# Selective scan: B held in two buffers and loaded ahead of C, constants and delta weights loaded where they are used

## The chip, the cores and the metric

The kernel runs on one core of a Trainium2 chip. The core has a matrix engine (TensorE, PE in the profile; its loads of stationary operands are PEld), a vector engine (VectorE, DVE), an engine for activation functions (ScalarE, ACT), a general engine (GpSimd, POOL), and SyncE (SP), whose queue issues nearly all transfers here. Each engine works through its own instructions in order; semaphores tie them together. Transfers between the device's DRAM and on-chip memory (SBUF) run on 16 DMA engines. The metric is the time of one execution on the device in microseconds (us); the profile is of one separate execution.

## What is computed

The reference is a stack of four residual layers on a picture batch x of 8 x 64 x 64 x 96 (float32). Each layer adds to x a function of its group norm. Layers 0 and 2 are selective scans, layer 1 is a chunked scan with one decay per head, layer 3 is a filter (upsampling by a Fourier transform, a small polynomial network, low pass). The change concerns above all layers 0 and 2, which have the same form:

```python
xz = x @ in_proj_w.T;  xp, z = split(xz)            # 192 channels each
xc = silu(depthwise_conv3x3(xp) + conv_b)           # u, as 4096 positions
xs = [rows, columns, rows backwards, columns backwards] of xc       # K = 4 directions
dts, B, C = split(x_proj_weight[k] @ xs[k])         # 6, 16 and 16 rows
delta = softplus(dt_projs_weight[k] @ dts + bias)   # 192 channels
for l in positions:                                 # state h: 192 channels x 16
    h = exp(delta[l] * A) * h + (delta[l] * u[l]) * B[l]
    y[l] = sum over the 16 states of h * C[l]
out = (layernorm(sum over directions of y + D * u) * silu(z)) @ out_proj_w.T
```

## The kernel before

The images are worked through one after the other; between the layers only the residual goes to DRAM and back. A selective layer (`selective_scan`) does 32 steps, one for each of the 4 directions and 8 chunks of `LC` = 512 positions. A step has six units (`units`, the variable `n`): a unit is 32 channels times 4 of the 16 states on the 128 partitions, and the other 4 groups of states (`NSG`) lie one behind the other in the free dimension, so that its tiles are 128 x 2048.

For each unit:

- `enter` (ACT, L528) copies the last states of the chunk before into the edge of `db`.
- `spread` (PE, L536) repeats delta * u of 32 channels on 128 partitions, into the PSUM tile `pu`, of which there is one. Units 2 and 5 use `du2` instead, which came through DRAM.
- `with_b` (L542) multiplies by B: `db = pu * b` on DVE for units 0, 1, 3 and 4, `db = du2 * b` on POOL for units 2 and 5.
- `decays` (ACT, L557) computes exp(A * delta) from `dx` into the PSUM tiles `das`, two halves of two instructions each.
- `scan` (DVE, L572) is the recurrence, two instructions per unit.
- `leave` (L588, L593) copies the last state on ACT and multiplies `h` by C in place on POOL; POOL's product waits for the copy.
- `total_y` (PE, L600 and L610) sums over the states for three units at a time; ACT copies the sum into `y` (L701).

What a step needs is made ahead by the generator `prepare(i)`. Each `yield` ends one part, and `prepare_part` runs one part. Two products on PE (L448, L458) with the joined weights `wdts` give the raw delta, B and C; ACT copies them to SBUF (`raw1` L453, `raw0` L463). B and C go to DRAM (`bcd`, L465) and come back repeated on partitions: `copies` (L472) issues four transfers of 256 KB each for `c` and four for `b`. Softplus (L483) makes delta; `dd` (L493, L495) takes it to DRAM by halves, and `repeat` (L490) brings each half back as a `dx` tile, four transfers of 192 KB each. `dx` of half 0 serves units 0 to 2, that of half 1 units 3 to 5. POOL multiplies delta by u (`du`, L501), and `dud` (L504) and `du2` (L507) take a part of that through DRAM.

The order of the work in this stage is written out by hand (`tc.manual_schedule()`): each engine gets its instructions in the order in which the program names them. The main loop runs over all units `t`; while step i runs, the parts of step i+1 are called at these places: parts 1 and 2 already in units 4 and 5 of the step before, part 3 in unit 1, parts 4 (`bcd` and `c`) and 5 (softplus, the first `dd`, `dx` of half 0, the second `dd`) in unit 2, part 6 (`b`) in unit 3, part 7 (`du`, `dud`, `du2`) in unit 4, part 8 (`dx` of half 1) in unit 5. All transfers of a step stand in this order in SP's queue. A transfer that reads DRAM that another one wrote waits on SP until that one has landed, and what stands behind it waits too.

Buffers come in pools. Those of `chunk` (`cp`: `c`, `dx`) have two buffers, those of `soft` (`tp`: `raw0`, `raw1`, `b`, `du`, `du2`, `wdts`) have one. `wdts`, the weights of all four directions, is loaded from DRAM at the start of the stage; `wdt` is computed once at the start of the program.

`cst`, a table of constants of 128 x 1746, lies in SBUF for the whole program. It holds the matrices that the selective scan uses (`sel`, `red`, `ident`), that of the group norm (`group`), those of the chunked scan (`tris`, `past`, `heads`, `sel6`, `same`, `lw_fixed`) and the filters of layer 3 (`up`, `down`). The chunked scan copies `lw_fixed` into `lw` at its start (L738), on DVE and POOL. Outside of the parts that are ordered by hand a scheduler orders the instructions.

Of the kernel before, what the change touches and what calls it, by code (L numbers as in the profile page):

```python
# [17 lines left out]
DM = 96  # L18
NST = 16
RK = 6  # L20
# [26 lines left out]
K_SEL = 0  # L47
K_RED = K_SEL + 128
K_ID = K_RED + 32
K_TF = K_ID + 128  # L50
K_TB = K_TF + 128
K_UF = K_TB + 128
K_UB = K_UF + 128
K_GRP = K_UB + 128
K_UP = K_GRP + 96
K_DN = K_UP + 128
K_LW = K_DN + 64
K_DIA = K_LW + 2 * LWC
K_S6 = K_DIA + 6
K_BLK = K_S6 + 4 * 96  # L60
K_ALL = K_BLK + 192


@with_exitstack
def tile_vision_stack(
# [26 lines left out]
        nc.sync.dma_start(t, src)  # L92
        return t

    cst = resident("cst", consts, [128, K_ALL])
    w0s = resident("w0s", w0, [DM, C_ALL])
    a0s = resident("a0s", a0, [128, K * 24])
    w1s = resident("w1s", w1, [DM, C_ALL])
# [6 lines left out]
    sel = cst[:DM, K_SEL:K_RED]  # L105
    red = cst[:, K_RED:K_ID]
    ident = cst[:, K_ID : K_ID + 128]
    tris = (cst[:, K_TF : K_TF + 128], cst[:, K_TB : K_TB + 128])
    past = (cst[:, K_UF : K_UF + 128], cst[:, K_UB : K_UB + 128])
    group = cst[:DM, K_GRP : K_GRP + 96]  # L110
    up = cst[:64, K_UP : K_UP + 128]
    down = cst[:, K_DN : K_DN + 64]
    lw_fixed = cst[:, K_LW : K_LW + 2 * LWC].rearrange("p (i r) -> p i r", i=2)
    heads = cst[:, K_DIA : K_DIA + RK]
    sel6 = cst[:, K_S6 : K_S6 + 4 * 96].rearrange("p (j m) -> p j m", j=4)
    same = cst[:DM, K_BLK : K_BLK + 192]

    zero = wp.tile([128, NSG], F32, name="zero")
    nc.vector.memset(zero, 0.0)
# [285 lines left out]
    def selective_scan(w, wdt, a, d, u, y):  # L405
# [18 lines left out]
            for c in (range(NCH) if k < 2 else range(NCH - 1, -1, -1))  # L424
        ]
        units = NCG
        total = len(steps) * units
        with (
            tc.tile_pool(name="dram", bufs=2, space=DRAM) as dp,
# [10 lines left out]
            def prepare(i):  # L440

                k, c = steps[i]
                wh, at = k % 2 == 1, c * LC
                uv = [view(u[:, hf, :], wh, at, LC) for hf in range(2)]
                m = made[i] = {"dx": [], "du": []}
                pv = pyp.tile([128, LC], F32, name="pv", tag="py")
                for hi in range(2):
                    nc.tensor.matmul(  # L448
                        pv[:DM], wdts[:, k, hi, 128:], uv[hi], start=(hi == 0), stop=(hi == 1)
                    )  # L450
                yield
                raw1 = tp.tile([128, LC], F32, name="raw1")
                nc.scalar.copy(raw1[:DM], pv[:DM])  # L453
                yield

                pv = pyp.tile([128, LC], F32, name="pv", tag="py")
                for hi in range(2):
                    nc.tensor.matmul(  # L458
                        pv, wdts[:, k, hi, :128], uv[hi], start=(hi == 0), stop=(hi == 1)
                    )  # L460
                yield
                raw0 = tp.tile([128, LC], F32, name="raw0")
                nc.scalar.copy(raw0, pv)  # L463
                bcd = dp.tile([32, LC], F32, name="bcd")
                nc.sync.dma_start(bcd, raw0[DM:])  # L465

                def copies(at, pool, name):

                    t = pool.tile([128, NSG, LC], F32, name=name)
                    src = bcd[at : at + NST].rearrange("(g n) l -> n g l", n=4)  # L470
                    for n in range(4):
                        nc.sync.dma_start(  # L472
                            t[32 * n : 32 * n + 32],
                            src[n : n + 1].to_broadcast([32, NSG, LC]),
                        )
                    return t

                m["c"] = copies(NST, cp, "c")
                yield
                delta = [raw0[:DM], raw1[:DM]]  # L480
                for hf in range(2):
                    bias = w[:, C_DTB + 2 * k + hf : C_DTB + 2 * k + hf + 1]
                    nc.scalar.activation(delta[hf], delta[hf], AF.Softplus, bias=bias)  # L483
                dd = dp.tile([192, LC], F32, name="dd")

                def repeat(hf):
                    dx = cp.tile([128, 3, LC], F32, name="dx")
                    src = dd[hf * 96 : hf * 96 + 96].rearrange("(q c) l -> c q l", c=32)
                    for n in range(4):
                        nc.sync.dma_start(dx[32 * n : 32 * n + 32], src)  # L490
                    m["dx"].append(dx)

                nc.sync.dma_start(dd[:DM], delta[0])  # L493
                repeat(0)
                nc.sync.dma_start(dd[DM:], delta[1])  # L495
                yield
                m["b"] = copies(0, tp, "b")
                yield
                du = tp.tile([DM, 2, LC], F32, name="du")
                for hf in range(2):  # L500
                    nc.gpsimd.tensor_mul(cut(du[:, hf, :], wh), cut(delta[hf], wh), uv[hf])  # L501
                m["du"] = du
                dud = dp.tile([32, 2, LC], F32, name="dud")
                nc.sync.dma_start(dud, du[64:96])  # L504
                m["du2"] = du2 = tp.tile([128, 2, LC], F32, name="du2")
                for n in range(4):
                    nc.sync.dma_start(du2[32 * n : 32 * n + 32], dud)  # L507
                yield
                repeat(1)
# [115 lines left out]
                    next(going[i], None)  # L625


            wdts = tp.tile([DM, K, 2, 224], F32, name="wdts")
            nc.sync.dma_start(wdts, wdt)
            dg = cp.tile([128, NSG, LC], F32, name="c").rearrange("p a b -> p (a b)")  # L630
            dg = dg[:DM, : 18 * DM].rearrange("p (n m) -> p n m", n=18)
            diagonals(dg, w)
# [4 lines left out]
            with tc.tile_pool(name="p_conv", bufs=2, space=PSUM) as pvp:  # L637

                def conv_block(n):
                    acc = pvp.tile([DM, 2, LC], F32, name="acc")  # L640
                    for hf in range(2):
                        conv_pe(dg, y, n, hf, acc[:, hf, :])
                    return n, acc

                def silu_block(n, acc):
                    for hf in range(2):
                        silu(w, u, (8 * n, 8 * n + 8), hf, acc[:, hf, :])

                for hf in range(2):
                    conv(w, y, u, (0, 8), hf)  # L650
                for _ in range(5):
                    prepare_part(0)
                blocks = [conv_block(5)]
                conv(w, y, u, (8, 24), 0)
                for _ in range(3):
                    prepare_part(0)
                conv(w, y, u, (8, 24), 1)
                for _ in range(2):
                    prepare_part(1)
                blocks.append(conv_block(6))  # L660
                silu_block(*blocks[0])
                conv(w, y, u, (24, 40), 0)
                blocks.append(conv_block(7))
                silu_block(*blocks[1])
                conv(w, y, u, (24, 40), 1)
                silu_block(*blocks[2])
            with tc.tile_pool(name="p_da", bufs=1, space=PSUM) as pap:
# [11 lines left out]
                for t in range(total + 2):  # L679
# [31 lines left out]
                    if n == 2:  # L711
                        prepare_part(i + 1)
                        prepare_part(i + 1)
                    elif n == 3:
                        prepare_part(i + 1)
                    elif n == 5:
                        prepare_part(i + 1)
                        prepare_part(i + 2)

    def chunked_scan(w, d, u, y):  # L720

        xproj = w[:, C_XP : C_XP + K * 2 * XR].rearrange("p (k j r) -> p k j r", k=K, j=2)
        yr = y.rearrange("p j (h w) -> p j w h", w=64)
        with tc.tile_pool(name="both", bufs=1) as bo, tc.tile_pool(name="bcd", bufs=1, space=DRAM) as bdp:
            lw = bo.tile([128, 2, NQ, LWC], F32, name="lw")
            for i in range(2):
                (nc.gpsimd.tensor_copy if i else nc.vector.tensor_copy)(  # L738
                    lw[:, i, :, :], lw_fixed[:, i : i + 1, :].to_broadcast([128, NQ, LWC])
                )  # L740

            bts = [bo.tile([DM, 4 * Q], F32, name=f"bt{n}") for n in range(2)]
            for bt in bts:
                nc.gpsimd.memset(bt, 0.0)
            bcds = [bdp.tile([32, L], F32, name=f"bcd{k}") for k in range(K)]
            for o in range(2):
                with tc.tile_pool(name="order", bufs=1) as op:
                    chunked_order(o, w, d, xproj, u, y, yr, lw, bts, bcds, op)

    def chunked_order(o, w, d, xproj, u, y, yr, lw, bts, bcds, op):  # L750
        xt = op.tile([128, NQ, 192], F32, name="xt")
        xd = op.tile([128, NQ, 2, RK + NST], F32, name="xd")
        dt = op.tile([128, NQ, 2, RK], F32, name="dt")
# [331 lines left out]
    def spectral_layer(xd, sb, dst):  # L1085

        with tc.tile_pool(name="spec", bufs=1) as lp, tc.tile_pool(name="spec2", bufs=2) as sp:
            xs = load(lp, xd)
            xn = lp.tile([DM, L], F32, name="xn")
            xt = lp.tile([64, 64, DM], F32, name="xt", tag="turn")  # L1090
            x1 = lp.tile([64, 128, DM], F32, name="x1")
# [287 lines left out]
```

## Time and profile before

| | |
|---|---|
| median of 3 runs | 32874.29 us (32872.7 to 32905.18) |
| the profiled execution's own time | 32765.36 us |
| its span in the profile | 32763.6 us |
| instructions | 279135 |
| DVE busy | 24776.0 us, 76% |
| PE busy | 24399.9 us, 74% |
| POOL busy | 21606.8 us, 66% |
| ACT busy | 16308.8 us, 50% |
| moved by DMA | 2684.51 MB, 82 GB/s on average |
| granted TensorE clock | 0.726 |

The span is the time from the first to the last instruction of one profiled execution. An engine's busy time leaves out its waits. The profile also gives, for each group of equal instructions, the time that the engine stood idle just before them and what ended it (the releaser); a list of waits, summed over the program; the instructions in order of time; and the time from a transfer's issue to its landing. For transfers, what the timeline shows under SPq is the issue alone, not the movement of the data.

### The profile page before, as it was taken

Reading aid. Unit: us, or ns where it says so; the run is one execution under the profiler, and the core shown is the slowest. Engines: PE = TensorE matmul, PEld = TensorE weight load, DVE = VectorE, ACT = ScalarE, POOL = GpSimd, SP = SyncE. Lnnn points to the kernel's source line nnn. Section 1 sums busy time; section 2 is a strip of 40 time slices with the busy share of each in tenths; the row PEclk is TensorE's granted clock in tenths of the full one; section 3 lists DMA queues with packets and bytes.
Section 4 is the critical chain, followed back from the end, with each engine's and each line's share of the span. In section 5 each row is a group of like instructions: output and inputs, shape, how many; then the busy total and the mean of one; then the engine's idle time right before and its main releaser. Section 6 shows DMA issues by size and latency. Waiting matters only on the chain. (4 is left out here: it accounts for less than half of the span.)

```text
span 32763.6 us, 279135 instructions
## 1 busy us (share of the span) xinstructions
PE 24399.9 (74%) x90246; PEld 9157.0 (28%) x90246; DVE 24776.0 (76%) x17921; ACT 16308.8 (50%) x28493; POOL 21606.8 (66%) x8844
## 2 busy tenths in 40 slices
PE   6696866968669686696766967669676686866868
PEld 1241311413114131141321413114131241312413
DVE  8858688586885868858688586886868868687686
ACT  5435454354543545435454354543545435454354
POOL 8639487394863948639477394864948639486494
PEclk7676776767767677677776767767677676776767
DMA  4314243042430424304243042431424314243142
GB/s 115 88 27 119 63 112 88 25 119 65 112 88 24 121 65 112 88 23 121 65 108 92 23 121 65 112 88 27 119 64 112 88 27 121 62 115 85 28 121 61
DMA packets 1496292, 2684.51 MB, mean 82 GB/s; under 512 B 304601, under 2 KB 304825, under 8 KB 1494833
## 3 DMA queue, kind: packets, MB, share of 16 engines
q1 hardware_dynamic: 1478192, 2660.35, 32.6%
q8 instruction: 722, 11.83, 0.2%
q10 hardware_dynamic: 16640, 6.29, 0.1%
q14 instruction: 738, 6.04, 0.1%
HBM read 2282.63 MB, written 383.06 MB: 81 GB/s over the span
## 5 line engine op out<-in xcount | busy, mean ns | idle before, releaser
L572 DVE TENSOR_TENSOR_SCAN h<-da,db 128x1026 f32<-128x1026 f32 x6144 | 13651.3, 2278 | 210.0
L593 POOL TENSOR_TENSOR h<-h,c 128x2048 f32<-128x2048 f32 x3072 | 12784.8, 4169 | 620.3 <-ACT state L588 490.6
L536 PE MATMUL pu<-du,cst 32*128 32x512 f32 x4096 | 3574.0, 966 | 5275.1 <-DVE db L542 5222.9
L542 DVE TENSOR_TENSOR db<-pu,b 128x2048 f32<-128x2048 f32 x2048 | 4654.1, 2272 | 2062.5 <-DMA b<-bcd 2057.1
L557 ACT ACTIVATE da<-dx,a2s 128x512 f32<-128x512 f32 x6144 | 4237.7, 690 | 3657.5 <-DVE h L572 3177.7
L557 ACT ACTIVATE da<-dx,a0s 128x512 f32<-128x512 f32 x6144 | 4237.7, 690 | 3639.4 <-DVE h L572 3156.5
L542 POOL TENSOR_TENSOR db<-du,b 128x2048 f32<-128x2048 f32 x1024 | 4648.7, 4540 | 1705.4 <-PE pu L536 644.8
L610 PE MATMUL py<-h,cst 128*32 128x512 f32 x24576 | 5307.4, 801 | 61.0 <-POOL h L593 61.0
L536 PEld LDWEIGHTS pu<-du,cst 32*128 32x128 f32 x4096 | 869.7, 263 | 7680.6 <-DVE db L542 6472.7
L610 PEld LDWEIGHTS py<-h,cst 128*32 128x32 f32 x24576 | 1150.6, 143 | 4882.5 <-issue 4778.8
L448 PE MATMUL pv<-u,wdts 96*96 96x512 f32 x2048 | 1461.5, 841 | 1101.7 <-ACT state L588 567.6
L237 POOL TENSOR_SCALAR xn<-xs,sb 96x512 f32<-96x512 f32 x192 | 207.2, 1084 | 3141.4 <-DVE sb L217 2960.3
L950 ACT ACTIVATE sg<-sg 128x768 f32<-128x768 f32 x1024 | 819.2, 800 | 2446.8 <-PE sg L934 2446.8
L881 POOL TENSOR_TENSOR rr<-lr,cst 128x768 f32<-128x768 f32 x256 | 430.3, 1681 | 2346.0 <-ACT lr L879 1252.2
L458 PE MATMUL pv<-u,wdts 96*128 96x512 f32 x2048 | 1504.1, 864 | 585.2 <-ACT state L588 325.5
L600 PE MATMUL py<-y,cst 96*96 96x512 f32 x1536 | 1551.3, 1108 | 39.6 <-ACT state L588 39.6
L501 POOL TENSOR_TENSOR du<-raw,u 96x512 f32<-96x512 f32 x1024 | 1435.4, 1423 | 0.0
L982 DVE TENSOR_TENSOR wt<-wt,cbm 128x768 f32<-128x768 f32 x1024 | 1089.1, 1084 | 344.6 <-ACT wt L951 341.3
L1020 PE MATMUL py<-wt,xdt 128*32 128x128 f32 x12288 | 1020.1, 332 | 236.1 <-DVE y L1058 156.6
L1028 PE MATMUL py<-ce,state 96*96 96x128 f32 x3968 | 1119.1, 372 | 0.0
L1141 DVE SCALAR_TENSOR_TENSOR f<-p,w3bs,f 128x512 f32<-128x512 f32 x768 | 576.8, 751 | 714.3 <-ACT f L1134 687.7
L588 ACT COPY state<-h 128x4 f32<-128x4 f32 x3072 | 592.8, 193 | 1017.1 <-DVE h L572 1008.7
(210 smaller groups left out, 32009.2 us busy)
## 6 DMA issues: line engine op xcount, KB each, us to landing
dx<-dd SPq DMA_DIRECT2D x4096, 192.0 KB, 3.7
c<-bcd SPq DMA_DIRECT2D x2048, 256.0 KB, 4.9
b<-bcd SPq DMA_DIRECT2D x2048, 256.0 KB, 6.3
du<-dud SPq DMA_DIRECT2D x2048, 128.0 KB, 2.6
dd<-raw SPq DMA_DIRECT2D x1024, 192.0 KB, 5.1
dud<-du SPq DMA_DIRECT2D x512, 128.0 KB, 6.2
xd<-xs SPq DMA_DIRECT2D x256, 192.0 KB, 2.0
xs<-xd SPq DMA_DIRECT2D x128, 384.0 KB, 5.8
```

The costliest lines, as they stand in the source:

```text
L448: nc.tensor.matmul(pv[:DM], wdts[:, k, hi, 128:], uv[hi], start=(hi == 0), stop=(hi == 1))
L458: nc.tensor.matmul(pv, wdts[:, k, hi, :128], uv[hi], start=(hi == 0), stop=(hi == 1))
L501: nc.gpsimd.tensor_mul(cut(du[:, hf, :], wh), cut(delta[hf], wh), uv[hf])
L536: nc.tensor.matmul(pu, sel[rows, :], m["du"][rows, n // 3, :], start=True, stop=True)
L542: (nc.gpsimd if pool else nc.vector).tensor_mul(groups(m["db", n]), (m["du2"][:, n // 3, :] if pool else m["pu"]) .unsqueeze(1) .to_broadc ...
L557: nc.scalar.activation(dst[:, g, :LC], made[i]["dx"][n // 3][:, n % 3, :], AF.Exp, scale=av4[:, k, n, gs : gs + 1],)
L572: nc.vector.tensor_tensor_scan(made[i]["h", n][:, at][:, way], das[p][:, rev : 2 * SEG + rev][:, way], made[i]["db", n][:, at][:, way], 0. ...
L593: nc.gpsimd.tensor_mul(h, h, made[i]["c"])
L600: nc.tensor.matmul(py, skip[:, hf, :] if k == 0 else ident[:DM, :DM], view((u if k == 0 else y)[:, hf, :], wh, c * LC, LC), start=True, st ...
L610: nc.tensor.matmul(py[32 * q : 32 * q + 32, :], red, hs[q][:, g, :], start=False, stop=(g == NSG - 1),)
L982: nc.vector.tensor_mul(it["wt"], it["wt"], m["cbm"][:, j : j + 1, :].to_broadcast([128, RK, Q]),)
L1028: nc.tensor.matmul(py[:, i, hf, :], it["before"][:, 96 * hf : 96 * hf + 96], m["ce"][:, j, :], start=False, stop=True,)
```

## The change

There are three parts, which hang together through the space in SBUF.

B: `b` moves from the pool with one buffer to that with two, and its four transfers move from a part of their own (part 6) to part 4, ahead of those of `c`. `prepare` has seven parts instead of eight, so one call at the start of the stage and the call in unit 3 fall away; all other parts stay in the units where they were.

Delta weights: instead of one load of 672 KB with all four directions at the start of a stage, one direction of 168 KB is loaded at a time, into two buffers `wk`. The first is loaded in the first part of step 0, the others in the first part of steps 2, 10 and 18, each six steps before its first use.

Constants: `cst` keeps only the 384 columns that selective scan and group norm use. Those of the chunked scan (1170 columns) are loaded as `cc` at the start of each chunked scan, the filters (192 columns) as `filters` at the start of layer 3, after `xs`. The columns of the table are reordered for it.

```diff
-    cst = resident("cst", consts, [128, K_ALL])
+    cst = resident("cst", consts[:, :K_TF], [128, K_TF])
...
             def prepare(i):
...
+                if i in (0, 2, NCH + 2, 2 * NCH + 2):
+
+                    j = (i + NCH - 1) // NCH
+                    weights[j] = cp.tile([DM, 2, 224], F32, name="wk")
+                    nc.sync.dma_start(weights[j], wdt[:, j])
                 pv = pyp.tile([128, LC], F32, name="pv", tag="py")
                 for hi in range(2):
                     nc.tensor.matmul(
-                        pv[:DM], wdts[:, k, hi, 128:], uv[hi], start=(hi == 0), stop=(hi == 1)
+                        pv[:DM], weights[k][:, hi, 128:], uv[hi], start=(hi == 0), stop=(hi == 1)
                     )
...
+                m["b"] = copies(0, cp, "b")
                 m["c"] = copies(NST, cp, "c")
                 yield
...
                 nc.sync.dma_start(dd[DM:], delta[1])
-                yield
-                m["b"] = copies(0, tp, "b")
                 yield
                 du = tp.tile([DM, 2, LC], F32, name="du")
...
-            wdts = tp.tile([DM, K, 2, 224], F32, name="wdts")
-            nc.sync.dma_start(wdts, wdt)
...
                 conv(w, y, u, (8, 24), 0)
-                for _ in range(3):
+                for _ in range(2):
                     prepare_part(0)
...
                     if n == 2:
                         prepare_part(i + 1)
                         prepare_part(i + 1)
-                    elif n == 3:
-                        prepare_part(i + 1)
                     elif n == 5:
...
     def chunked_scan(w, d, u, y):
...
+            cc = bo.tile([128, K_UP - K_TF], F32, name="cc")
+            nc.sync.dma_start(cc, consts[:, K_TF:K_UP])
+            lw_fixed = cc[:, K_LW - K_TF : K_DIA - K_TF].rearrange("p (i r) -> p i r", i=2)
...
     def spectral_layer(xd, sb, dst):
...
             xs = load(lp, xd)
+            filters = lp.tile([128, 192], F32, name="filters")
+            nc.sync.dma_start(filters, consts[:, K_UP:])
+            up, down = filters[:64, :128], filters[:, 128:]
```

`chunked_order` takes `cc` as an argument and cuts `tris`, `past`, `heads`, `sel6` and `same` out of it, as was done with `cst`.

More of the change, by code (lines that the diff above doesn't have):

```diff
@@ L49 @@
 K_ID = K_RED + 32
-K_TF = K_ID + 128
+K_GRP = K_ID + 128
+K_TF = K_GRP + 96
 K_TB = K_TF + 128
@@ L53 @@
 K_UB = K_UF + 128
[L54 to L57, printed above, removed]
+K_LW = K_UB + 128
 K_DIA = K_LW + 2 * LWC
@@ L60 @@
 K_BLK = K_S6 + 4 * 96
-K_ALL = K_BLK + 192
+K_UP = K_BLK + 192
+K_DN = K_UP + 128
+K_ALL = K_DN + 64
 @with_exitstack
@@ L107, in tile_vision_stack @@
     ident = cst[:, K_ID : K_ID + 128]
-    tris = (cst[:, K_TF : K_TF + 128], cst[:, K_TB : K_TB + 128])
-    past = (cst[:, K_UF : K_UF + 128], cst[:, K_UB : K_UB + 128])
     group = cst[:DM, K_GRP : K_GRP + 96]
[L111 to L116, printed above, removed]
     zero = wp.tile([128, NSG], F32, name="zero")
@@ L426, in selective_scan @@
         units = NCG
+        weights = {}
         total = len(steps) * units
@@ L458, in prepare @@
                     nc.tensor.matmul(
-                        pv, wdts[:, k, hi, :128], uv[hi], start=(hi == 0), stop=(hi == 1)
+                        pv, weights[k][:, hi, :128], uv[hi], start=(hi == 0), stop=(hi == 1)
                     )
@@ L747, in chunked_scan, with chunked_order, part @@
                 with tc.tile_pool(name="order", bufs=1) as op:
-                    chunked_order(o, w, d, xproj, u, y, yr, lw, bts, bcds, op)
-    def chunked_order(o, w, d, xproj, u, y, yr, lw, bts, bcds, op):
+                    chunked_order(o, w, d, xproj, u, y, yr, cc, lw, bts, bcds, op)
+    def chunked_order(o, w, d, xproj, u, y, yr, cc, lw, bts, bcds, op):
+        def part(at, n):
+            return cc[:, at - K_TF : at - K_TF + n]
+        tris = (part(K_TF, 128), part(K_TB, 128))
+        past = (part(K_UF, 128), part(K_UB, 128))
+        heads = part(K_DIA, RK)
+        sel6 = part(K_S6, 4 * 96).rearrange("p (j m) -> p j m", j=4)
+        same = part(K_BLK, 192)[:DM]
         xt = op.tile([128, NQ, 192], F32, name="xt")
```

## The prediction

> **What bounds the kernel now.** I began with the page's engine shares: DVE 76%, PE 74%, POOL 66%, so no engine is full on average. I then asked for busy times by stretch.
>
> ```profile
> span 32763.6 us, 279135 instructions
> 122.00:1396.00 1274.00, 841.11 (x2140) 190.60 (x2140) 1133.18 (x511) 754.38 (x1394) 1160.72 (x317) 0.69 0.47 117
> L593 POOL TENSOR_TENSOR h<-h,c 128x2048 f32<-128x2048 f32 x3072 | 12784.8, 4169 | 620.3 <-ACT state L588 490.6
> ```
>
> The second line is one selective-scan stage (stretch and its length; then busy us of PE, PEld, DVE, ACT, POOL; clock, DMA share, GB/s). There are 16 of them (8 images, layers 0 and 2), some 20,400 us of the span. A stage has 32 steps. POOL works 1160.72/32 = 36.3 us of each, DVE 1133.18/32 = 35.4, and a step takes 40.06 us (the distance between the first scans of neighbouring steps, a mean over all 496 of them). So about 4 us of each step is nobody's work. The list of waits names it:
>
> ```profile
> DVE db L542 <- DMA b<-bcd: 2057.1, 496, 6.1
> ACT da L557 <- DMA dx<-dd: 757.0, 490, 3.5
> ```
>
> DVE waits for b 496 times, once in every step but the first of a stage: 2057.1/496 = 4.15 us. ACT waits for dx as often, 1.5 us, which costs nothing today since DVE waits longer. One step in order of time (start, duration; gaps in brackets):
>
> ```profile
> 1021.47 0.31 SPq L465 DMA_DIRECT2D bcd<-raw  x1
> 1023.12 1.73 SPq L472 DMA_DIRECT2D c<-bcd  x4
> 1023.78 4.53 POOL L542 TENSOR_TENSOR db<-du,b 128x2048 f32<-128x2048 f32 x1
> 1024.95 0.38 SPq L493 DMA_DIRECT2D dd<-raw  x1
> ...
> 1030.49 1.72 SPq L490 DMA_DIRECT2D dx<-dd  x4
> ...
> 1032.31 0.37 SPq L495 DMA_DIRECT2D dd<-raw  x1
> ...
> 1032.79 1.90 SPq L472 DMA_DIRECT2D b<-bcd  x4
> ...
> 1034.88 8.27 POOL L593 TENSOR_TENSOR h<-h,c 128x2048 f32<-128x2048 f32 x2
> ...
> 1036.15 1.42 ACT L557 ACTIVATE da<-dx,a0s 128x512 f32<-128x512 f32 x2 [1.70 <-DMA dx<-dd]
> ...
> 1036.23 2.07 PE L536 MATMUL pu<-du,cst 32*128 32x512 f32 x2
> ...
> 1041.32 2.29 DVE L542 TENSOR_TENSOR db<-pu,b 128x2048 f32<-128x2048 f32 x1 [4.13 <-DMA b<-bcd]
> ...
> 1043.71 4.48 DVE L572 TENSOR_TENSOR_SCAN h<-da,db 128x1026 f32<-128x1026 f32 x2
> ```
>
> The reader is to see three things. The transfers of a step run nose to tail from 1023 to 1048. b's last reader (POOL's db) is done at 1028.31, so b is issued at 1032.79 not because its buffer is late but because it stands behind dx, which waits on SP for dd to land. And dx lands for ACT at 1036.15, five us before b does.
>
> [...] the first dd, 192 KB behind c, is issued at 1024.95 and lets dx go at 1030.49, 5.5 us later, while bcd, 64 KB with an empty queue, lets c go after 1.65. [...] the second buffer of b is needed to issue it at 1023.12, but the bubble now comes from b's place in the queue. [...] POOL's h*c is 4.17 us beside a busy DVE (at 1028.28) and 8.27/2 = 4.14 beside an idle one. So I keep all durations when work moves together.
>
> **The change part by part.** *b ahead of c.* b's four issues come to 1023.12, c's four follow them, and dd, dx and the second dd come after. b then lands where c lands now, before dd lets dx go at 1030.49, and DVE's wait for b is gone: 4.13 us at most per step. But b is 1.05 MB (4 x 256 KB) and it is now ahead of dd and dx. By slices of a us, c and dd moved at 156, 283, 236, 211, 236 and 125 GB/s: 1.247 MB in some 5.3 us, 235 GB/s. At this rate b takes 4.46 us; at the 225 GB/s of the stretch with dx, dd, b and dud (2.16 MB in 9.6 us) it takes 4.66. I take 4.5. The eight issues (1.73 us per four) are over at 1026.6, before the data, so they add nothing to it. So dd lands 4.5 us later (dx is issued at 1035.0 and not 1030.49), dx lands 4.5 later, and ACT's first pair of exponentials starts at 1036.15 + 4.5 = 1040.65. It ends 1.42 later, at 1042.07, and the scan follows by 1042.1. Now it starts at 1043.71. **Gain per step: 1.6 us, not 4.1.** What is late next is dx.
>
> *Is anything later than dx?* DVE's last scan ends at 1037.19; pu is ready at 1036.23 + 2.07 = 1038.3; db takes 2.29, so the scan could start at 1040.7. PE is 1.4 us ahead of dx. POOL: behind ACT's wait for dx stands the copy of state (L588, 0.2), for which the last h*c of the step waits; behind that h*c stand POOL's db, three h*c, db, h*c and du. h*c then starts at 1042.3 (now about 1039.0) and ends at 1046.5; du2, issued when dud has landed, is in by about 1046 as it is now. Until du is done: 4.54 + 3 x 4.17 + 4.54 + 4.17 + 3.0 = 28.8, at 1075.3. The next pu follows by 1077.3 and db by 1079.7, where dx allows the next scan at 1042.1 + 38.45 = 1080.5. So POOL has 0.8 us left and dx decides. raw1's copy on ACT (L453), behind the same wait, goes to about 1044.5; PE's y (L600) needs that buffer and moves by 0.5 us, inside its cover until ACT's copy at 10.5 us of the step.
>
> *Weights.* 16 loads of 672 KB become 64 of 168 KB. The first of a stage now waits until the space of the projection is free (about 2340 in the second stage shown by the timeline, where it was issued at 2308.97), and lands some 2.5 us later; two PE products (L448, from 2340.57) move by about 2 us. PE stands 4.66 us at 2354 for POOL's diagonals, which hides it; uncovered it is 16 x 2.5 = 40 us. The other 48 loads stand before dud, 168 KB or 0.75 us each; POOL is then busy with h*c; uncovered 36 us.
>
> *Constants.* cc (585 KB: 2.6 us, and 1.6 as bcd needs) is loaded 8 times before the chunked scan. Its readers are the two lw copies; DVE's now has six more conv operations of 1.28 us before it, so it waits for nothing; uncovered 8 x 4.2 = 34 us. filters (96 KB) comes behind xs and is read only after the transposes. The first cst load is 585 + 96 KB smaller: 3 us once. In the chunked layer's convolution the same operations stand in another order on DVE; I take 0, and +-50 us in all for that and for space that comes free at other times.
>
> **Sum.** 496 steps x 1.6 = 794 us. Profiled span 32763.6 - 794 = 31,970 (its own time is 32,765.36). The median of the runs is 32,874.29, 0.33% above that; I take the same 794 off: **32,080 us**, 2.4% faster.
>
> **Rivals.** *The whole wait goes* (496 x 4.13 = 2,050, so 30,825): for it speaks the waits list, against it pu at 1038.3; it can't be. Its real form is that b hardly delays dx, by less than 3.1 us, and pu bounds: 1043.71 - 1040.7 = 3.0 us, 1,490 us, 31,385; POOL's 36.3 us of work and its waits don't allow more. For it: eight transfers queued together might run faster than four. Against: the stretch with dx, dd and b queued together ran at 225 GB/s, no faster. *Slower:* b delays dx by more than 1043.71 - 1037.57 = 6.1 us; from there dx takes more than b cost. b's own median from issue to landing is 6.3 us, but most of that is dx ahead of it. [...] *No effect:* the built kernel's list of instructions has b ahead of c in every step and no wait for DVE or POOL on it, so this is out, save where the delay happens to be 6.1 +- 0.13.
>
> **How the numbers follow.** dx bounds with a delay of 3.9 to 5.1 us: 0.62 (gain 1.0 to 2.2 us, 31,780 to 32,380). Less delay, pu or POOL bound: 0.16 (31,385 to 31,780). More delay, still faster: 0.12 (32,380 to 32,808). No change: 0.03. Slower: 0.07. A range of 31,450 to 32,500 leaves out about half of the 0.12, a little of the 0.16, and the last two cases, under 2 in 10. Faster by over 0.2% (66 us, about what a measurement of this kernel can tell) 0.90, same 0.03, slower 0.07.
>
> **What would show it.** In the profile after: DVE's wait for b gone from the list; in its place a wait of DVE for ACT's da before the first scan of a step, some 1.5 us; ACT's wait for dx grown from 1.5 us to about 4.5; a step of 38.4 us; 8.3 us and not 5.5 from the first dd's issue to dx's; POOL over 94% busy in the stage. Wrong: dx issued less than 3.5 us or more than 6 after its place now, or a step near 37 with POOL's waits for ACT gone.

## The result, and the profile after

| | before | after |
|---|---|---|
| median of the runs (4 each) | 32874.01 us (32872.7 to 32905.18) | 32370.09 us (32279.72 to 32413.18) |
| ratio, 95% interval | | 0.9841 [0.9818, 0.9864] |
| profiled execution, its own time | 32765.36 us | 32341.96 us |
| its span | 32763.6 us | 32340.2 us |
| mean step of a selective stage | 40.06 us | 39.24 us |
| predicted | | 32,080 us, which is a ratio of 0.9758; range 31,450 to 32,500 |

The kernel is 1.6% faster, where 2.4% was forecast: the side and the range hold, the size does not. The span is 423.4 us shorter. The 16 selective stages, timed in the trace, went from 1275.3 to 1250.0 us each, which is 16 x 25.3 = 404 us. Everything else together is 19 us, with parts of either sign: the chunked part lost 9 us in each image, the last spectral layer grew by 20. In the other kernels run here the same parts move by as much from one execution to the next (999 to 1017 us and 430 to 452 us), so none of it is put down to an edit. One caution on all figures per step: the profiled execution of before is 109 us (0.33%) shorter than the median of its runs, that of after only 28. By the medians the gain is 504 us, which would be 1.02 us per step if all of it lay in the steps. So a difference to the profile of before can be off by some 0.2 us per step.

A step (the distance from one first scan to the next, mean over 496) gained 0.82 us. The forecast was 1.6. From the page after: its first line, the scan's group (busy us and mean ns; idle time before it and what ended most of that), and busy times by stretch for the first selective stage (columns as before).

```profile
span 32340.2 us, 279752 instructions
L569 DVE TENSOR_TENSOR_SCAN h<-da,db 128x1026 f32<-128x1026 f32 x6144 | 13650.9, 2278 | 1504.6 <-ACT da L554 1343.0
120.00:1368.00 1248.00, 853.37 (x2140) 219.93 (x2138) 1131.88 (x511) 752.78 (x1394) 1158.31 (x317) 0.69 0.52 120
```

The scan's line in the page before:

```profile
L572 DVE TENSOR_TENSOR_SCAN h<-da,db 128x1026 f32<-128x1026 f32 x6144 | 13651.3, 2278 | 210.0
```

The work is what it was: 2278 ns for a scan, 1131.88 us of DVE and 1158.31 of POOL in the stage against 1133.18 and 1160.72. Only idle time went: 1274 us became 1248. The scan now waits for `da`, which before it hardly did (210.0 us of idle time in all, against 1504.6). The list of waits (total us, times, longest us):

```profile
ACT da L554 <- DMA dx<-dd: 3324.1, 474, 9.4
DVE h L569 <- ACT da L554: 1343.0, 504, 5.8
DVE db L539 <- PE pu L533: 378.4, 271, 1.7
POOL h L590 <- issue: 1363.7, 496, 6.4
```

DVE's wait for b, 2057.1 us before, is gone from the list. In its place stand 1343.0/504 = 2.7 us per step for ACT's exponentials, and those wait 3324.1/474 = 7.0 us for dx, against 1.5 before. POOL's h*c is held up once a step (496 times). The profile names no releaser for it ("issue"); that it stands behind the same wait is read from the order of work, in which ACT copies the state for it right after these exponentials. One step in order of time:

```profile
1002.06 1.73 SPq L470 DMA_DIRECT2D b<-bcd  x4
...
1003.89 1.85 SPq L470 DMA_DIRECT2D c<-bcd  x4
...
1006.03 0.31 SPq L492 DMA_DIRECT2D dd<-raw  x1
...
1014.74 1.72 SPq L489 DMA_DIRECT2D dx<-dd  x4
...
1015.18 2.07 PE L533 MATMUL pu<-du,cst 32*128 32x512 f32 x2
...
1017.28 2.29 DVE L539 TENSOR_TENSOR db<-pu,b 128x2048 f32<-128x2048 f32 x1 [1.15 <-PE pu L533]
...
1020.53 1.41 ACT L554 ACTIVATE da<-dx,a0s 128x512 f32<-128x512 f32 x2 [7.13 <-DMA dx<-dd]
...
1021.98 4.48 DVE L569 TENSOR_TENSOR_SCAN h<-da,db 128x1026 f32<-128x1026 f32 x2 [2.40 <-ACT da L554]
...
1022.20 4.18 POOL L590 TENSOR_TENSOR h<-h,c 128x2048 f32<-128x2048 f32 x1 [3.06 <-issue]
```

b stands where c stood. DVE's `db` is done at 1019.57, and the scan still has to wait until 1021.98, because dx was issued at 1014.74 and ACT could start only at 1020.53. From the first dd's issue to dx's it is 8.7 us here, 5.5 before.

To say where the rest of the gain went, I read the landings of each transfer from the trace, in us after the first scan of the step that prepares them (medians over the steps):

| lands at | before | after | later by |
|---|---|---|---|
| first 256 KB behind bcd | 23.01 (c) | 23.17 (b) | |
| the fourth | 26.49 (c) | 26.97 (b) | |
| the eighth | | 31.75 (c) | |
| first dd | 26.73 | 32.04 | 5.31 |
| last of the first dx | 32.10 | 37.59 | 5.49 |

The forecast had dd and dx 4.5 us later. They are 5.3 to 5.5 later. So the mechanism is as argued and one size is off, by about as much as the missing gain. Two questions are left: is it really the place in the queue, and why do 1.05 MB cost more than 4.5 us?

### The profile page after: what moved, and what is told of

Read it like the earlier page. It is cut to its first block, busy times and chain, and to the rows that moved or that the text cites. A ratio compares the mean times of both kernels' runs of the same rounds, so it can differ in the third digit from the quotient of the medians.

```text
span 32340.2 us, 279752 instructions
## 1 busy us (share of the span) xinstructions
PE 24628.1 (76%) x90246; PEld 9665.8 (30%) x90246; DVE 24740.3 (77%) x17921; ACT 16289.9 (50%) x28493; POOL 21607.3 (67%) x8844
## 5 line engine op out<-in xcount | busy, mean ns | idle before, releaser
L569 DVE TENSOR_TENSOR_SCAN h<-da,db 128x1026 f32<-128x1026 f32 x6144 | 13650.9, 2278 | 1504.6 <-ACT da L554 1343.0
L590 POOL TENSOR_TENSOR h<-h,c 128x2048 f32<-128x2048 f32 x3072 | 12773.0, 4172 | 1463.2 <-issue 1363.7
L607 PE MATMUL py<-h,cst 128*32 128x512 f32 x24576 | 5446.8, 798 | 93.9 <-POOL h L590 93.9
L607 PEld LDWEIGHTS py<-h,cst 128*32 128x32 f32 x24576 | 1619.7, 142 | 4584.5 <-issue 3239.5
L446 PE MATMUL pv<-u,wk 96*96 96x512 f32 x2048 | 1484.1, 854 | 1131.0 <-ACT state L585 564.1
L885 POOL TENSOR_TENSOR rr<-lr,cc 128x768 f32<-128x768 f32 x256 | 433.3, 1693 | 2254.2 <-ACT lr L883 1203.7
L456 PE MATMUL pv<-u,wk 96*128 96x512 f32 x2048 | 1529.9, 877 | 442.4 <-ACT state L585 249.6
```

The costliest lines, as they stand in the source:

```text
L446: nc.tensor.matmul(pv[:DM], weights[k][:, hi, 128:], uv[hi], start=(hi == 0), stop=(hi == 1))
L456: nc.tensor.matmul(pv, weights[k][:, hi, :128], uv[hi], start=(hi == 0), stop=(hi == 1))
L569: nc.vector.tensor_tensor_scan(made[i]["h", n][:, at][:, way], das[p][:, rev : 2 * SEG + rev][:, way], made[i]["db", n][:, at][:, way], 0. ...
L590: nc.gpsimd.tensor_mul(h, h, made[i]["c"])
L607: nc.tensor.matmul(py[32 * q : 32 * q + 32, :], red, hs[q][:, g, :], start=False, stop=(g == NSG - 1),)
```

## The experiments

Each edit is against the changed kernel unless it says otherwise. All ratios are to the kernel before, run beside it.

**The buffer without the place (e1).** b has its two buffers, and the weights and constants are as in the change, but b's transfers are issued where they were, behind the second dd.

```diff
-                m["b"] = copies(0, cp, "b")
                 m["c"] = copies(NST, cp, "c")
...
                 yield
+                m["b"] = copies(0, cp, "b")
+                yield
                 du = tp.tile([DM, 2, LC], F32, name="du")
...
+                    elif n == 3:
+                        prepare_part(i + 1)
```

> The changed kernel, but b is issued where it was before (a part of its own behind the second dd, called in unit 3); it keeps its two buffers, and constants and weights stay as changed. Theory (the place in the queue decides, not the buffer): DVE waits for b as before, 4.1 us a step, a step of 40.0 us, and the time is that of before, 32,790 to 32,900 us. Rival (the second buffer brings the gain): the time of the changed kernel, about 32,370.

Measured 32957.01 us, ratio 1.0035 [1.0025, 1.0046], step 40.53 us. From its list of waits:

```profile
DVE db L540 <- DMA b<-bcd: 2288.3, 496, 6.6
ACT da L555 <- DMA dx<-dd: 924.9, 491, 4.2
```

The wait for b is back, 496 times: the second buffer alone buys nothing, and the place in the queue is what counts. What I did not expect is that it is slower than before: b is waited for 2288.3 us instead of 2057.1, 0.47 us more per step by the profiles (by the medians of the runs, 32957.01 against 32832.70, it is 0.25), with the same transfers in the same order. Something makes the transfers themselves slower; what it is comes out below.

**c ahead of b (e2).** The two `copies` change places; all eight transfers still stand ahead of dd.

> The changed kernel with c's four transfers ahead of b's, both ahead of the first dd. Theory (only what stands ahead of dd counts; b lands by 31.8 us of the step and is wanted at 34.3): nothing changes, a step of 39.2 us, 32,300 to 32,420 us. Rival (b has to be ahead of c): DVE waits for b again, the time goes back to 32,600 or more.

Measured 32250.15 us, 0.9814 [0.9794, 0.9834], step 39.10. Its wait of the scan:

```profile
DVE h L569 <- ACT da L554: 1270.1, 504, 5.3
```

Nearly the changed kernel's 1343.0. Which of the two comes first makes no difference that these runs can tell; that both are ahead of dd is what sets the time.

**One of c's four transfers behind dx (e3).** `copies` is given a range of transfers: three stay, the fourth goes behind the first dx.

```diff
-                m["c"] = copies(NST, cp, "c")
+                m["c"] = copies(NST, cp, "c", range(3))
...
                 repeat(0)
+                copies(NST, cp, "c", (3,), m["c"])
                 nc.sync.dma_start(dd[DM:], delta[1])
```

> The changed kernel with the last of c's four transfers (256 KB) moved behind the first dx. Theory (dx sets the step, and each 256 KB ahead of dd delays it by some 1.25 us): a step of 38.0 us, 496 x 1.25 = 620 us less than the changed kernel, 31,750 us. Rival (at 39.2 us the step has come to what PE, POOL or the sum of all transfers allow): no gain, 32,370.

Measured 31753.15 us, 0.9663 [0.9639, 0.9686], step 38.07. From its waits:

```profile
ACT da L555 <- DMA dx<-dd: 2778.4, 478, 8.4
DVE h L570 <- ACT da L555: 739.0, 494, 4.8
```

256 KB less ahead of dd takes 39.24 - 38.07 = 1.17 us off the step, and the scan's wait falls by (1343.0 - 739.0)/496 = 1.22. By the table above one of c's transfers takes (31.75 - 26.97)/4 = 1.20 us. The step follows what stands ahead of dd one for one, so dx is the bound. The landings say it more sharply. In the changed kernel, in its second run below, in e2, e3, e5, e6 and e10, the next step's first scan starts 1.57 us after the last of the first dx has landed, with a standard deviation of 0.04 to 0.05 over the steps. In the kernel before and in e1, e8 and e9 it starts 2.53 to 2.54 us after the last of b (0.05 to 0.07). Each kernel hangs on one of the two landings.

**All of c behind du2 (e4).** Only b stays ahead of dd; c's four transfers come last but for the second dx.

```diff
                 m["b"] = copies(0, cp, "b")
-                m["c"] = copies(NST, cp, "c")
                 yield
...
                     nc.sync.dma_start(du2[32 * n : 32 * n + 32], dud)
+                m["c"] = copies(NST, cp, "c")
                 yield
```

> The changed kernel with all four transfers of c moved behind du2, so that b alone stands ahead of dd as c alone did before. Theory: dx lands where it did before, 5 us earlier than in the changed kernel, and pu on PE and POOL's 36.3 us of work bound the step at 36.7 to 37.2 us: 31,130 to 31,370 us. Rival 1 (the step is at its bound already): 32,370. Rival 2 (c now comes too late for the first h*c on POOL): a step of over 38 us, 31,800 or more.

Measured 31081.15 us, 0.9461 [0.9439, 0.9483], step 36.70: 5.4% faster than before, and ahead of both kernels. The first selective stage by busy times, its waits, and a piece of its timeline:

```profile
120.00:1290.00 1170.00, 850.47 (x2140) 208.68 (x2140) 1130.80 (x511) 753.24 (x1394) 1157.24 (x317) 0.71 0.55 128
```

```profile
DVE db L539 <- PE pu L533: 400.8, 299, 1.6
POOL h L590 <- DMA c<-bcd: 11.6, 23, 1.2
DVE h L569 <- ACT da L554: 9.7, 20, 0.7
```

```profile
442.77 8.33 POOL L590 TENSOR_TENSOR h<-h,c 128x2048 f32<-128x2048 f32 x2
...
451.03 4.56 POOL L539 TENSOR_TENSOR db<-du,b 128x2048 f32<-128x2048 f32 x1
...
455.51 12.47 POOL L590 TENSOR_TENSOR h<-h,c 128x2048 f32<-128x2048 f32 x3
```

The scan's wait is down to 9.7 us in the whole program. POOL is busy 1157.24 of the stage's 1170 us, 99%, and its operations stand edge to edge; DVE with 1130.80 us, 97%, comes close behind. c, though moved some ten transfers back, is late by only 11.6 us in all: its first reader is h*c of the next step. So c does not have to be ahead of dd, and what bounds now is POOL's work. With c out of the way the step is 3.36 us shorter than before (40.06 - 36.70), most of the 4.15 us for which DVE had waited; with c in the way it is 0.82. Whether moving c alone would have done as much, with b left in its old place, was not tried.

**Why is b dearer than 4.5 us?** e1's loss, with nothing but buffers, weights and constants different from before, pointed away from the queue. The addresses of the built kernels offer a suspect. `cst` lost 1362 columns, 5448 bytes on each partition (5472 by the addresses), and with it every tile behind it moved: in the kernel before, `c` and `dx` start at multiples of 512 bytes and `b` at a multiple of 256; in the changed one all three start 160 bytes past a multiple of 512. That the start of a tile bears on the time of its loads was a guess of the author's. To test it, an unused tile ahead of the others shifts them all:

```diff
+    pad = wp.tile([128, 88], F32, name="pad")
+    nc.vector.memset(pad, 0.0)
     row = wp.tile([128, DM], F32, name="row")
```

88 columns (352 bytes) bring b, c and dx to multiples of 512 (e5); 8 columns (32 bytes) only to multiples of 64 (e6); 24 columns (96 bytes) to odd multiples of 256 (e10). The unaltered changed kernel ran beside e5 and e6; e10 ran later, beside e8 and e9, so its ratio to before is what compares.

> The changed kernel itself, unaltered, as the base for the three beside it: a step of 39.1 to 39.3 us, 32,230 to 32,410 us.

> The changed kernel with an unused tile of 352 bytes per partition ahead of the selective scan's pools, which only shifts addresses: b, c and dx then begin at multiples of 512 bytes, as c and dx did before the change (in the changed kernel they begin 160 bytes past such a multiple). Theory A (the change made each transfer some 5% slower by shifting where it lands): 256 KB take 1.17 to 1.20 us in the stream, dx lands 0.5 us earlier, a step of 38.5 to 38.8 us, 31,990 to 32,200 us. Theory B (b and c in one stream of eight are slower whatever the address): a step of 39.1 to 39.3, 32,230 to 32,410 us.

> As the run before, but a shift of 32 bytes only: b, c and dx begin at a multiple of 64 bytes, but 192 bytes past a multiple of 256 or 512. Theory A with 64 bytes as the grain: as in the aligned run, 31,990 to 32,200 us. Theory A with a coarser grain, or theory B: as the changed kernel, 32,230 to 32,410 us.

> The changed kernel shifted by 96 bytes: b, c and dx begin at an odd multiple of 256 bytes. If 256 bytes are the grain: as with the shift of 352 bytes, a step of 38.8 us, 32,080 to 32,160 us. If 512 are: as the changed kernel, 39.2 us, 32,230 to 32,410 us.

| tiles start at | median, us | ratio to before | step, us |
|---|---|---|---|
| 160 past a multiple of 512 (the change) | 32298.99 | 0.9827 [0.9813, 0.9842] | 39.20 |
| 192 past a multiple of 256 (e6) | 32316.55 | 0.9832 [0.9815, 0.9848] | 39.18 |
| odd multiples of 256 (e10) | 32134.81 | 0.9769 [0.975, 0.9789] | 38.78 |
| multiples of 512 (e5) | 32126.03 | 0.9773 [0.9758, 0.9788] | 38.78 |

The step is 38.78 us at the odd multiples of 256 and at the multiples of 512, 0.42 less than the 39.20 of the changed kernel; at 192 past a multiple of 256, which is a multiple of 64, it is 39.18. Multiples of 128 that are not multiples of 256 were not tried. One step of e5's queue:

```profile
1034.63 0.32 SPq L494 DMA_DIRECT2D dd<-raw  x1
...
1042.53 1.72 SPq L491 DMA_DIRECT2D dx<-dd  x4
```

It takes 7.9 us from dd to dx, but this step is a short one: over all steps the median is 8.33 in e5 and 8.71 in the changed kernel. The eight landings of b and c go from 23.11 to 31.36 us of the step, 8.25/7 = 1.18 us apart, where the changed kernel takes from 23.17 to 31.75, 8.58/7 = 1.23.

Does the same hold where the order of the transfers is the old one? The kernel before, with 40 columns of padding so that `c` and `dx` come to lie 160 past a multiple of 512 (e8), and e1 with the 352 bytes (e9):

> The kernel before with an unused tile of 160 bytes per partition ahead of the pools, so that c and dx begin 160 bytes past a multiple of 512 bytes, as in the changed kernel; nothing else. Theory (address alone costs some 3% of each transfer): DVE waits 0.4 us longer for b, a step of 40.5 us, 33,050 to 33,130 us. Rival (the loss of the run with b in its old place came from the weights or the constants): 32,850 to 32,910 us.

> b in two buffers but in its old place, as in the first experiment, and the shift of 352 bytes that brings b, c and dx back to multiples of 512 bytes. Theory: the time of before, a step of 40.0 to 40.1 us, 32,790 to 32,900 us. Rival (buffer, weights or constants cost something of their own): 32,950 us or more.

Measured: e8 33144.27 us, 1.0087 [1.0058, 1.0115], step 40.64. e9 32833.73 us, 0.9977 [0.9967, 0.9987], step 40.23. The wait for b, first in e8, then in e9:

```profile
DVE db L544 <- DMA b<-bcd: 2337.5, 496, 7.0
```

```profile
DVE db L542 <- DMA b<-bcd: 2136.0, 496, 6.8
```

The kernel before becomes 0.9% slower by nothing but an unused tile: its wait for b grows from 2057.1 to 2337.5 us, 0.57 us per step, and its step by 0.58 (0.48 by the medians of the runs, 33144.27 against 32908.50). Aligned, e1 is back at the time of before, if anything a little under it; that its profiled step (40.23) stays 0.17 above that of before is within what the quick profiled execution of before explains. So the second buffer, the weights and the constants together cost nothing that a run can tell, and e1's loss is the address. e8 and e9, which ran beside each other, are 0.4 us per step apart, as much as the changed kernel and e5.

The traces also hold the single pieces of 2 KB, and these settle where the time goes. Taken from 1.2 us before the first landing of the transfers between bcd and dd to 0.3 us before the last, over all steps, a piece is on its DMA engine for this long on average:

| order of the transfers | 160 past a multiple of 512 | 192 past (e6) | odd multiples of 256 (e10) | multiples of 512 |
|---|---|---|---|---|
| c alone ahead of dd | 143.9 ns (e1), 143.7 (e8) | | | 135.7 (before), 135.4 (e9) |
| b and c ahead of dd | 153.1 ns (after) | 154.1 | 145.5 | 145.5 (e5) |

The pieces are as large and, but for a few in 1.5 million, as many in e5 as in the changed kernel; each one takes 5 to 6% longer on average at the two starts tried that are no multiple of 256 (153.1 and 154.1 against 145.5 ns; in the old order 143.9 and 143.7 against 135.7 and 135.4). The padding also moves tiles that dd and dud read, and all that the engines use; but these pieces are c's and b's, which come from DRAM, so of the addresses that they touch it moves only the written one. A placement of each tile by itself was not tried.

**Both together (e7).** e4 with 352 bytes.

> c's transfers behind du2 (as in the run with c behind) and the shift of 352 bytes together. Theory: dx is no longer what bounds, POOL and DVE are (DVE has 35.9 us of work and POOL up to 37.2 in a step), so the address brings next to nothing: a step of 36.6 to 36.7 us, 30,980 to 31,100 us. Rival (transfers still bound): 0.5 us less per step, 30,850.

Measured 31093.19 us, 0.9457 [0.9439, 0.9475], step 36.70; e4 has 31081.15 us and 36.70. In this kernel, where POOL bounds, the shift brings nothing that these runs can tell.

## Why the prediction was right, and where it was off

*DVE's wait for b goes.* Right: gone from the list. e1 shows that the second buffer alone brings nothing of this: it comes with the place in the queue. Whether the place would do it with one buffer was not tried; the prediction took the second one to be needed, since b's last reader ends only at 1028.31.

*b delays dd and dx, and dx bounds.* Right: e3 moves the bound by moving 256 KB past dx, e4 takes it away, and the first scan follows dx's last landing by 1.57 us in every kernel that dx bounds.

*The size of that delay: "I take 4.5". This is the term that failed.* It measured 5.31 us at dd and 5.49 at dx. The forecast's 1.6 us of gain were what 4.5 left of a margin of 6.1, which was read from one step; over all steps of before, the first scan starts 7.83 us after dx's last landing, which is 6.3 us more than the 1.57 that it needs. 6.3 - 5.5 = 0.8, and 0.82 was measured. So the error in the delay cost 1.0 us, and a margin that was 0.2 wider than the step shown made up for a part of it by luck.

The delay that was missed has two parts. With aligned tiles dx's last landing comes 0.47 us earlier (37.59 in the changed kernel, 37.12 in e5), and the step is 0.42 shorter (39.20 to 38.78). The prediction did not look at this: it had listed the constants as space and as loads, not as what the addresses of all other tiles hang on. The other part is there even when aligned: dx's last landing in e5 is 5.0 us later than before, and 4.8 later than in e9, which has the old order and e5's padding (37.12 - 32.33; at dd 31.63 - 26.82). Four transfers at the steady pace of e5 are 4 x 1.18 = 4.7 us; the last 0.1 to 0.3 is left open. The rate of 235 GB/s that gave 4.46 was a mean over a stretch with the stream's fast first part in it (283 GB/s in one slice). Over all steps of before, in slices of a us from 20.5 us after the first scan, the DMA engines moved 179, 277, 219, 226, 224 and 102 GB/s, so only the start is quick. What was added here in the middle of a full queue paid the steady pace, 262 KB in 1.18 us aligned and 1.23 not, which is 222 and 213 GB/s. The 225 GB/s that the prediction also had, and set aside, was nearer.

*pu and POOL next.* Right for pu: DVE waits 1.15 us for it in the step shown (forecast 1038.3 - 1037.19 = 1.1), and e4, where dx no longer bounds, waits for it 299 times, 1.3 us each. POOL's 0.8 us of margin in the cycle was not used up in the changed kernel; in e4 POOL is the bound. The rival "b hardly delays dx", 31,385 us, would have needed a delay under 3.1 us and is out.

*The h\*c of the last unit behind ACT's wait for dx.* It waits where that was forecast: POOL's line L590 waits in 496 steps, 2.7 us on average (1363.7/496), 3.06 in the step shown. That ACT's copy is what holds it is read from the order alone.

*Slower, if the delay is over 6.1 us.* It came to 5.3 to 5.5, with a margin of 6.3. Two more losses the size of the address (0.42 us per step) would have taken all that was left, so this rival was not far off.

*What would show it.* The scan's wait for `da` was to be 1.5 us and is 2.7 over the program (2.40 in the step shown): the same delay that was too small, since this wait is dx's lateness seen from DVE. ACT's wait for dx was to be 4.5 and is 7.0: here the prediction lost a sum, for 1.5 there before and 4.5 more are 6.0; with the delay of 5.5 it is the 7.0 measured. 8.7 us from dd to dx, against 8.3. POOL 1158.31/1248 = 92.8% busy and not over 94%: a longer step for the same work.

*Two readings of the trace before.* The transfers do not run quite nose to tail: the DMA engines moved nothing from 1030 to 1031 us and from 1041 to 1042, while SP waited for dd and for dud to land. And the two h*c of 4.14 us do not stand beside an idle DVE: it was idle for 4.13 of their 8.27 us only. What was drawn from this, that durations stay when work moves, holds here: the scan took 2278 ns before and after, and h*c took 4169 ns on average before, 4172 in the changed kernel and 4187 in e4, where DVE is 97% busy in the stage.

*Weights and constants at nothing.* Right in sum. PE waits 18.6 us for `wk` in the whole program (7 waits). POOL stands 24.0 us in 8 waits for `cc`, ahead of its `lw` copy, which the prediction had not looked at; DVE's copy waits for nothing, as forecast. Nothing of it is seen in the chunked part, which did not get longer, and e9 finds no cost of these edits together. The +-50 us kept for order and space held the 19.

## What to carry to other kernels

A transfer that was moved ahead in the queue here was paid for by what stood behind it (b's 1.05 MB ahead of it, at the new starts, made dd land 5.31 us later and the first dx 5.49); before such a move, list for each transfer in the queue when its first reader wants it, and order by that (here c was wanted last and stood early, and moving it back took the ratio from 0.984 to 0.946). Price an addition to a full queue by the pace between neighbouring landings in its middle (here 1.18 and 1.23 us per 256 KB), not by the mean of a burst (4.46/4 = 1.12 at the 235 GB/s of the forecast). And when a tile is taken out of SBUF, look at where the others come to start: here a padding tile of 96 bytes took the ratio from 0.983 to 0.977.

## What the runs showed of the hardware

In these kernels the pace of the loads of b and c changed with the start of the tiles in SBUF. With pieces of 2 KB (512 positions of float32), the transfers of 256 KB between bcd and dd landed 1.23 us apart at starts 160 bytes past a multiple of 512, and 1.18 at multiples of 512; a piece took 153.1 and 145.5 ns on average. Odd multiples of 256 gave the same step as multiples of 512 (both 38.78 us), and 192 past a multiple of 256 about the same as 160 past 512 (39.18 and 39.20); other starts were not tried. In the two kernels whose queue sets the pace this was 0.5% (32298.99 to 32126.03 us) and 0.9% (the kernel before, shifted); in the one that POOL bounded it was nothing that the runs can tell (31081.15 and 31093.19 us).
